# One step of a softplus moved from VectorE to ScalarE, and a buffer of its own for B and C

## The chip, the cores and the metric

The kernel runs on one core of a Trainium2 chip. Its engines take instructions from queues of their own, in order, and wait for one another by semaphores: TensorE (PE; its weight loads are PEld), VectorE (DVE), ScalarE (ACT), GpSimd (POOL) and SyncE (SP), which here only issues DMAs. SBUF is the on-chip memory, and PSUM the memory that TensorE writes its products to. The metric is device microseconds of one execution, lower is better.

## What is computed

Two layers act on x, (4, 128, 64, 64) in fp32. Layer 0 is a selective scan over four orders of the pixels (rows, columns, and both reversed); layer 1, an additive attention and a recurrence, is not touched. Of layer 0 the part that matters, for each image and each of the K = 4 orders:

```python
dt = softplus(dts + dt_bias)           # per channel and pixel
def step(h, inp):                      # along the L = 4096 pixels of the order
    ut, dtt, bt, ct = inp
    dA = jnp.exp(dtt[..., None] * A)   # N = 16 states per channel
    h = dA * h + (dtt * ut)[..., None] * bt
    y = jnp.sum(h * ct, axis=-1)
    return h, y
```

The kernel takes the softplus of s as relu(s) + ln(1 + e), with e = exp(-|s|). In fp32, 1 + e is rounded; to make up for that it adds the error of the rounding, e - ((1 + e) - 1). So four terms are summed: e, relu(s), minus ((1 + e) - 1), and ln(1 + e).

## The kernel before, in words

Layer 0 is cut into 64 items: 4 images by 4 orders (i = 0 to 3) by 4 chunks of CH = 1024 pixels. An item is 16 units, v = 0 to 15, each a pair of (four of the 16 states) by (32 of the 128 channels), so that one unit fills 128 partitions by 1024. The text below calls item m's units v0, v1 and so on.

One unit u goes through the engines so. `decay` (L624): ACT writes dA = exp(dt * A) to a PSUM tile `pa`, of which there are two. `entering` (L629): POOL writes dBu = dtdu * B to one of three buffers. `scan` (L644): DVE runs the recurrence along the 1024 pixels, with the last column of the item before (`carry`) as its start; then, in 10 of 16 units, DVE multiplies by C into a buffer `h` (L651); in the other 6, v2, v5, v7, v10, v13 and v15, the scan writes `h` itself and POOL multiplies it by C (L654). There are five `h` buffers. ACT copies the last column to `carry` (L652), and the POOL multiplication comes after that copy. `collect` (L669 and L671): once per two units TensorE adds their `h` into the sum `py`; the first two of an item (after v3 and v5) also add the skip term or the order before (L669). `deliver` (L678, at v2) copies the finished sum of the item before out of `py`.

Beside that, one step per unit, the inputs of item m + 2 are prepared during item m (the tuple `Item.STEPS`, L594):

- v0 `inputs`: TensorE projects B and C. v1 `outputs` (L554): ACT copies them to `bc`, and a DMA on SP's queue (L556) writes `bc` to DRAM, from where it is spread to all partitions later (L607).
- v2 `raw`: TensorE projects s. v3 `signs` (L567, L568): ACT takes |s| to `e` and relu(s) to `dd`. v4 `power` (L571): ACT makes e = exp(-|s|).
- v5 `first`: TensorE starts a sum in PSUM with identity * e and identity * dd.
- v6 `second`: DVE makes `ec` = (e + 1) - 1 (L579), then ACT overwrites e with ln(1 + e) (L580).
- v7 `third`: TensorE adds `nident` * ec, where `nident` is minus the identity, and identity * ln.
- v8 `products`: DVE multiplies by the source (L588), ACT copies dt (L590), and a DMA on SP's queue (L592) writes both to DRAM; four spreads per item (L599) bring them back for the units.

`bc` and `ec` share one buffer (tag "ec" of a pool with one buffer per tag): `bc` of one item may not be overwritten by `ec` before its DMA has read it.

All of this stands in one order written out by hand: the loop at L781 issues, for each unit u, decay(u+1), entering(u+2), perhaps `deliver`, the step of `STEPS` and other work put beside it (the layer's ending for the image before, normalisation and convolutions for the next), then scan(u), its `carry` copy and POOL's multiplication, then perhaps `collect`, then the DMAs. Each engine runs its share of that order in sequence.

Ahead of the loop, items 0 and 1 are prepared without overlap (L710 to L719): all steps of item 0, its spreads (24 DMAs, of which 16 are spreads of dt and 8 of B and C), then all steps of item 1, then four ACT copies that transpose the image (L454) with four DMAs (L460), and then the first `decay`.

Of the kernel before, what the change touches and what calls it, by code (L numbers as in the profile page):

```python
# [8 lines left out]
F32 = mybir.dt.float32  # L9
AF = mybir.ActivationFunctionType  # L10
ALU = mybir.AluOpType
# [4 lines left out]
P = 128  # L16
# [4 lines left out]
CH = 1024  # L21
K = 4
N = 16
# [121 lines left out]
@with_exitstack  # L145
def _bounded(
    ctx: ExitStack,
    tc: tile.TileContext,
    flag,
    x1,  # L150
    x, in_wT, conv_w, conv_b, sa_w, sa_b, xpT, xpR, dtwT, dtb, A_quads, Ds,
    on_g, on_b, n1_g, n1_b, out_wT, WtT, WxT, Wt, Wx, bh, Wa, ba, W, WT, VT, gamma, beta,
    out,
):
    nc = tc.nc
    const = ctx.enter_context(tc.tile_pool(name="fconst", bufs=1))
    dram = ctx.enter_context(tc.tile_pool(name="gdram", bufs=1, space=DRAM))
    k = _Consts(tc, const)
    x2 = dram.tile([B, P, L], F32, name="x2")

    with tc.manual_schedule():
        _layer0(tc, k, x, x1, in_wT, conv_w, conv_b, sa_w, sa_b, xpT, xpR, dtwT, dtb, A_quads, Ds,
                on_g, on_b, n1_g, n1_b, out_wT)
    top = const.tile([P, TOPS], F32, name="top")
    with tc.manual_schedule():
        _rational(tc, k, x1, x2, top, Wt, Wx, bh, Wa, ba)
    with tc.tile_pool(name="gresid", bufs=1) as resid:
        X = resid.tile([P, B, L], F32, name="X")
        for b in range(B):
            nc.sync.dma_start(X[:, b, :], x2[b])  # L170
        _chunked(tc, None, flag, top, X, k.ident, k.avg, k.ones, k.eps5, k.load, k.filled,
                 W, WT, VT, gamma, beta, out)
# [3 lines left out]
def _layer0(ctx, tc, k, x, x1, in_wT, conv_w, conv_b, sa_w, sa_b, xpT, xpR, dtwT, dtb, A_quads, Ds,  # L176
# [8 lines left out]
    nc = tc.nc  # L185
    load, filled, ident, avg, ones, eps5, eps6 = k.load, k.filled, k.ident, k.avg, k.ones, k.eps5, k.eps6
    wp = ctx.enter_context(tc.tile_pool(name="l0w", bufs=1))
# [7 lines left out]
    def pq():  # L195
        return psQ.tile([P, MM], F32, name="pq", tag="pq")
# [30 lines left out]

    skip = wp.tile([P, P], F32, name="skip")
    nc.vector.tensor_scalar(skip, ident, d_sum, None, ALU.mult)
    nident = wp.tile([P, P], F32, name="nident")  # L230
    nc.vector.tensor_scalar(nident, ident, -1.0, None, ALU.mult)


    gmat = filled(wp, [P, P], 0.25, "gmat")
# [62 lines left out]
    pp = ctx.enter_context(tc.tile_pool(name="l0prep", bufs=1))  # L297
# [13 lines left out]
    def banks(lhsT, src, start=True, stop=True, into=None):  # L311

        into = into or [pq() for _ in parts]
        if lhsT is not None:
            for ps, m in zip(into, parts):
                nc.tensor.matmul(ps, lhsT, src[:, m], start=start, stop=stop)
        return into
# [212 lines left out]
    class Item:  # L530
# [18 lines left out]
                nc.tensor.matmul(ps[0 : 2 * N, :], w_xp[:, self.i, :], self.src[:, m], start=True, stop=True)  # L549

        def outputs(self):
            bc = pp.tile([2 * N, CH], F32, name="bc", tag="ec")
            for ps, m in zip(self.ps, parts):
                nc.scalar.copy(bc[:, m], ps[0 : 2 * N, :])  # L554
            self.bcd = dram.tile([2 * N, CH], F32, name="bcd")
            nc.sync.dma_start(self.bcd, bc)  # L556
# [16 lines left out]
        def first(self):  # L573
            self.ps = banks(ident, self.e, stop=False)
            banks(ident, self.dd[:, 0, :], start=False, stop=False, into=self.ps)

        def second(self):
            self.ec = pp.tile([P, CH], F32, name="ec", tag="ec")
            nc.vector.tensor_scalar(self.ec, self.e, 1.0, 1.0, ALU.add, ALU.subtract)  # L579
            nc.scalar.activation(self.e, self.e, AF.Ln, bias=1.0)  # L580

        def third(self):
            banks(nident, self.ec, start=False, stop=False, into=self.ps)
            banks(ident, self.e, start=False, into=self.ps)

        def products(self):
# [5 lines left out]
            nc.sync.dma_start(self.ddd.rearrange("s d l -> d s l"), self.dd)  # L592

        STEPS = (inputs, outputs, raw, signs, power, first, second, third, products)  # L594

        def spread_dt(self, r):
# [1012 lines left out]
```

## Time and profile before

| what | value |
|---|---|
| three runs | 11802.34, 11821.63, 11826.4 us; median 11821.63 |
| the profiled execution | 11810.23 us, its span 11808.5 us |
| span taken by layer 0 | to about 4069 us; its loop of units starts at 220.8 us |
| DVE, ACT, POOL, PE busy from 2000 to 3000 us | 906.47, 554.10, 865.69, 759.90 us |
| period of one item | 50.5 to 68.5 us; 55.8 us for many |
| L579 on DVE | 64 times, 149.4 us; shortest 664, median 1328, longest 7178 ns |

A row of the timeline gives the start and the duration in us, the engine, the line, the operation, output<-input with shapes, and in brackets how long the engine had been idle before it and what ended the wait. An item's period is the distance from its first scan to the next item's first scan. A duration may contain time in which the instruction was held up after it had been started.

### The profile page before, as it was taken

Reading aid. Unit: us, or ns where it says so; the run is one execution under the profiler, and the core shown is the slowest. Engines: PE = TensorE matmul, PEld = TensorE weight load, DVE = VectorE, ACT = ScalarE, POOL = GpSimd, SP = SyncE. Lnnn points to the kernel's source line nnn. Section 1 sums busy time; section 2 is a strip of 40 time slices with the busy share of each in tenths; the row PEclk is TensorE's granted clock in tenths of the full one; section 3 lists DMA queues with packets and bytes.
Section 4 is the critical chain, followed back from the end, with each engine's and each line's share of the span. In section 5 each row is a group of like instructions: output and inputs, shape, how many; then the busy total and the mean of one; then the engine's idle time right before and its main releaser. Section 6 shows DMA issues by size and latency. Waiting matters only on the chain.

```text
span 11808.5 us, 111596 instructions
## 1 busy us (share of the span) xinstructions
PE 10343.2 (88%) x36083; PEld 3200.5 (27%) x36083; DVE 9180.8 (78%) x10131; ACT 9429.7 (80%) x10096; POOL 8599.9 (73%) x3648
## 2 busy tenths in 40 slices
PE   5687787677776699999999999999999999999986
PEld 2121122122111133333333333333333333333324
DVE  4999899889989677777777777777777777777763
ACT  3455555555555599999999999999999999999985
POOL 2898889889889677767767776767677667767751
PEclk8898898889888899999999999999999999999998
DMA  4778778778778300000000000000000000000001
GB/s 107 180 180 193 172 175 187 171 174 188 178 168 189 87 1 3 6 3 3 6 3 3 3 6 3 3 3 6 3 3 6 3 2 3 4 2 2 4 17 43
DMA packets 224900, 737.83 MB, mean 62 GB/s; under 512 B 41056, under 2 KB 42016, under 8 KB 223792
## 3 DMA queue, kind: packets, MB, share of 16 engines
q1 hardware_dynamic: 221184, 729.96, 26.2%
q8 instruction: 285, 4.67, 0.2%
q14 instruction: 311, 2.55, 0.1%
q10 hardware_dynamic: 3120, 0.64, 0.0%
HBM read 613.01 MB, written 117.44 MB: 62 GB/s over the span
## 4 chain that ended last, share of the span: by engine, by line
PE 49%; ACT 10%; DVE 4%; issue 3%; POOL 0%; DMA 0%; DVEq 0%; POOLq 0%; SPq 0%; ACTq 0%
PE pn L1215 26%; PE pd L1215 15%; ACT A L1384 3%; PE ct L1360 3%; ACT A L1385 2%; DVE rb L1230 2%; ACT rb L1234 1%; ACT rb L1235 1%; PE ct L1137 1%; ACT ra L1234 1%; PE wxs L1501 0%; DVE A L1346 0%; DVE rb L1242 0%; PE pn L55 0%; PE ct L1265 0%
## 5 line engine op out<-in xcount | busy, mean ns | idle before, releaser
L1215 PE MATMUL pn<-cE,F 32*128 32x512 f32 (+1 forms) x12288 | 4724.9, 649 | 193.1 <-DVE rb L1230 85.4
L1230 DVE TENSOR_TENSOR rb<-rb,pn 128x512 f32<-128x512 f32 x3972 | 2543.1, 682 | 1310.3 <-PE pd L1215 684.2
L1215 PE MATMUL pd<-E,F 32*128 32x512 f32 (+1 forms) x12288 | 3474.6, 648 | 24.7 <-DVE ra L1242 19.5
L1349 POOL TENSOR_TENSOR ra<-ra,rb 128x1024 f32<-128x1024 f32 x993 | 2634.3, 2653 | 953.1 <-DVE rb L1230 952.7
L1336 POOL TENSOR_TENSOR ra<-ra,rb 128x1024 f32<-128x1024 f32 x993 | 2347.5, 2364 | 407.1 <-DVE rb L1230 347.2
L629 POOL TENSOR_TENSOR dBu<-dtdu,bbcc 128x1024 f32<-128x1024 f32 x1024 | 2398.2, 2368 | 273.8 <-DMA dtdu<-ddd 154.1
L1235 ACT ACTIVATE rb<-rb 128x1024 f32<-128x1024 f32 x1986 | 2100.3, 1058 | 62.8
L1215 PEld LDWEIGHTS pn<-cE,F 32*128 32x128 f32 (+1 forms) x12288 | 1416.3, 185 | 2571.4 <-DVE rb L1230 1067.5
L1234 ACT ACTIVATE rb<-pd 128x1024 f32<-128x1024 f32 x1986 | 2007.7, 1011 | 83.2 <-PE pn L1215 69.9
L671 PE MATMUL py<-h,gather 128*32 128x512 f32 x4096 | 1304.2, 702 | 479.7 <-POOL h L654 381.8
L1230 DVE TENSOR_TENSOR ra<-ra,pn 128x512 f32<-128x512 f32 x1986 | 1315.6, 683 | 230.3 <-ACT ra L1235 183.9
L1215 PEld LDWEIGHTS pd<-E,F 32*128 32x128 f32 (+1 forms) x12288 | 930.6, 185 | 1642.4 <-issue 884.3
L624 ACT ACTIVATE pa<-dtdu,a_neg 128x1024 f32<-128x1024 f32 x1024 | 1144.9, 1118 | 52.4 <-DVE h L644 31.3
L654 POOL TENSOR_TENSOR h<-h,bbcc 128x1024 f32<-128x1024 f32 x384 | 924.1, 2406 | 351.2 <-ACT carry L652 343.7
L644 DVE TENSOR_TENSOR_SCAN pa<-pa,carry,dBu 128x1024 f32<-128x1024 f32 x480 | 1125.2, 2344 | 21.8 <-ACT pa L624 11.3
L1235 ACT ACTIVATE ra<-ra 128x1024 f32<-128x1024 f32 x993 | 1049.5, 1057 | 31.4
L1360 PE MATMUL ct<-A,xT 128*128 128x512 f32 x2048 | 1046.8, 639 | 11.1 <-ACT A L1385 11.0
L1234 ACT ACTIVATE ra<-pd 128x1024 f32<-128x1024 f32 x993 | 1008.8, 1016 | 59.4 <-PE pd L1215 27.4
L652 ACT COPY carry<-pa 128x1 f32<-128x1 f32 x640 | 102.4, 160 | 1120.8 <-DVE h L651 1119.4
L1346 DVE TENSOR_TENSOR A<-ra 128x512 f32<-128x512 f32 x993 | 743.4, 749 | 116.1 <-POOL ra L1336 115.7
L651 DVE TENSOR_TENSOR h<-pa,bbcc 128x1024 f32<-128x1024 f32 x640 | 783.8, 1225 | 60.4 <-DVE pa L644 1.8
L644 DVE TENSOR_TENSOR_SCAN h<-pa,carry,dBu 128x1024 f32<-128x1024 f32 x288 | 674.9, 2343 | 124.1 <-PE py L671 80.4
(286 smaller groups left out, 8832.5 us busy)
## 6 DMA issues: line engine op xcount, KB each, us to landing
bbcc<-bcd SPq DMA_DIRECT2D x1024, 256.0 KB, 7.0
dtdu<-ddd SPq DMA_DIRECT2D x1024, 256.0 KB, 7.1
ddd<-dd SPq DMA_DIRECT2D x64, 1024.0 KB, 5.1
src<-src SPq DMA_DIRECT2D x64, 512.0 KB, 8.1
xs<-in_x_dram SPq DMA_DIRECT2D x16, 512.0 KB, 7.5
src<-xs SPq DMA_DIRECT2D x16, 512.0 KB, 3.0
bcd<-bc SPq DMA_DIRECT2D x64, 128.0 KB, 2.1
src<-xsT SPq DMA_DIRECT2D x16, 512.0 KB, 4.4
```

The lines of the kernel that those rows point to most:

```text
L624: nc.scalar.activation(dA, its[m].DT[r][:, 0, :], AF.Exp, scale=a)
L629: nc.gpsimd.tensor_tensor(dBu, its[m].DT[r][:, 1, :], its[m].BC[q][:, 0, :], ALU.mult)
L644: nc.vector.tensor_tensor_scan(to[:, step], dA[:, step], live.pop(("dBu", u))[:, step], 0.0 if m % nch == 0 else its[m - 1].carry[:, col : ...
L654: nc.gpsimd.tensor_tensor(h, h, cc, ALU.mult)
L671: nc.tensor.matmul(it.y[to, c], gather, live["h", v][:, c], start=False, stop=(q == QS - 1))
L1215: nc.tensor.matmul(ps[a], F[lo:hi, i, jt * P : (jt + 1) * P], side[lo:hi, i, :], start=True, stop=True)
L1230: nc.vector.tensor_tensor(r[:, a, :], r[:, a, :], ns[a], ALU.mult)
L1234: nc.scalar.activation(r, d, AF.Ln, scale=LOWER)
L1235: nc.scalar.activation(r, r, AF.Exp, scale=-1.0)
L1336: nc.gpsimd.tensor_tensor(rA_, rA_, rB2_, ALU.add)
L1349: nc.gpsimd.tensor_tensor(rA, rA, rB1, ALU.add)
L1360: nc.tensor.matmul(ct, xT[:, jt, :], A[:, jt, :], start=(jt == 0), stop=(jt == JT - 1))
```

## The change

`second` loses its DVE instruction. In its place `first` issues two ScalarE activations after its matmuls: ec = 1 + e, and then ec = 1 - ec, which is minus ((1 + e) - 1). So `third` multiplies by the plain identity, and `nident` is gone. `bc` gets a buffer of its own.

```diff
-    nident = wp.tile([P, P], F32, name="nident")
-    nc.vector.tensor_scalar(nident, ident, -1.0, None, ALU.mult)
...
         def outputs(self):
-            bc = pp.tile([2 * N, CH], F32, name="bc", tag="ec")
+            bc = pp.tile([2 * N, CH], F32, name="bc")
...
             self.ps = banks(ident, self.e, stop=False)
             banks(ident, self.dd[:, 0, :], start=False, stop=False, into=self.ps)
 
+            self.ec = pp.tile([P, CH], F32, name="ec")
+            nc.scalar.activation(self.ec, self.e, AF.Identity, bias=1.0)
+            nc.scalar.activation(self.ec, self.ec, AF.Identity, scale=-1.0, bias=1.0)
+
         def second(self):
-            self.ec = pp.tile([P, CH], F32, name="ec", tag="ec")
-            nc.vector.tensor_scalar(self.ec, self.e, 1.0, 1.0, ALU.add, ALU.subtract)
             nc.scalar.activation(self.e, self.e, AF.Ln, bias=1.0)
 
         def third(self):
-            banks(nident, self.ec, start=False, stop=False, into=self.ps)
+            banks(ident, self.ec, start=False, stop=False, into=self.ps)
             banks(ident, self.e, start=False, into=self.ps)
```

In the built program's order of instructions, DVE lacks the 64 `ec` instructions and `nident`, ACT has 128 more and no further table load, and TensorE's, POOL's and SP's lists keep their length and order. On ACT the two stand between the decay of v6 and the carry copy of v5.

## The prediction, made before the changed kernel was run

> **What bounds the kernel now.** The slices come first, since the share of the whole span hides where the edit lies.
>
> ```profile
> DVE  4999899889989677777777777777777777777763
> ACT  3455555555555599999999999999999999999985
> POOL 2898889889889677767767776767677667767751
> ```
>
> Layer 0 is slices 1 to 14. There DVE and POOL are full and ACT is half idle, so work seems to be moved from a bound engine to a free one. But two engines are near full, and which of them ends an item has to be read per item. Next, the group and the waits of DVE (220 to 3985 us):
>
> ```profile
> L579 DVE TENSOR_SCALAR ec<-e 128x1024 f32<-128x1024 f32 x64 | 149.4, 2335 | 48.4 <-DMA bcd<-bc 35.5 <-ACT e L571 13.0
> ```
>
> ```profile
> DVE h L644 <- PE py L671: 94.3, 62, 3.9
> ```
>
> L579 takes 2335 ns in the mean, yet 664 at its shortest. Item by item, of the 62 inside the loop 28 take 0.66 to 0.67 us, 19 take 1.1 to 2.1, and 15 take 6.3 to 7.2. And DVE also waits for TensorE 62 times, always for an `h` buffer. Three places in the timeline tell what the durations mean. Item 17 (order i = 0):
>
> ```profile
> 1208.27 1.12 ACT L624 ACTIVATE pa<-dtdu,a_neg 128x1024 f32<-128x1024 f32 x1
> 1210.22 6.59 DVE L579 TENSOR_SCALAR ec<-e 128x1024 f32<-128x1024 f32 x1
> 1211.58 2.38 POOL L654 TENSOR_TENSOR h<-h,bbcc 128x1024 f32<-128x1024 f32 x1
> 1213.89 2.36 POOL L629 TENSOR_TENSOR dBu<-dtdu,bbcc 128x1024 f32<-128x1024 f32 x1
> 1216.73 2.35 DVE L644 TENSOR_TENSOR_SCAN pa<-pa,carry,dBu 128x1024 f32<-128x1024 f32 x1
> 1219.15 2.36 POOL L629 TENSOR_TENSOR dBu<-dtdu,bbcc 128x1024 f32<-128x1024 f32 x1 [2.90 <-DVE pa L644]
> 1220.32 2.34 DVE L644 TENSOR_TENSOR_SCAN h<-pa,carry,dBu 128x1024 f32<-128x1024 f32 x1
> ```
>
> L579 is held until POOL stops: POOL's last ends at 1216.25, L579 at 1216.81, 0.56 later. POOL stops only for lack of a dBu buffer, which the scan queued behind L579 would free: each holds up the other. Item 30 (i = 3):
>
> ```profile
> 1999.03 1.37 DVE L579 TENSOR_SCALAR ec<-e 128x1024 f32<-128x1024 f32 x1
> 1999.81 2.93 POOL L654 TENSOR_TENSOR h<-h,bbcc 128x1024 f32<-128x1024 f32 x1
> 2005.57 1.06 PE L671 MATMUL py<-h,gather 128*32 128x512 f32 x4
> 2006.76 2.35 DVE L644 TENSOR_TENSOR_SCAN h<-pa,carry,dBu 128x1024 f32<-128x1024 f32 x1 [2.77 <-PE py L671]
> ```
>
> Here the scan of v7 waits 2.77 us for TensorE's second sum, which ends at 2006.63. And the preparation of item 1, ahead of the loop:
>
> ```profile
> 195.49 0.31 SPq L556 DMA_DIRECT2D bcd<-bc  x1
> 204.22 0.69 DVE L579 TENSOR_SCALAR ec<-e 128x1024 f32<-128x1024 f32 x1 [35.45 <-DMA bcd<-bc]
> 204.97 3.78 PE L316 MATMUL pq<-ec,nident 128*128 128x512 f32 x4 [20.91 <-DVE ec L579]
> 220.78 2.30 DVE L644 TENSOR_TENSOR_SCAN pa<-pa,dBu 128x1024 f32<-128x1024 f32 x1 [8.64 <-ACT pa L624]
> ```
>
> `ec` waits for the shared buffer until the DMA has read `bc`, and that DMA stands on SP's queue behind 24 spreads. The whole loop starts late for it.
>
> **What the Trainium skill says.** "SBUF — State Buffer", Who interferes with whom: DVE in a mode that reads one tensor through both its ports locks the port pair that is GpSimd's only one, for the whole instruction, and the loser blocks fully; ACT waits for nobody. The trace agrees (the 0.56 us above; POOL's 2.93 beside its usual 2.36). The page's "whoever starts first" doesn't tell why 15 cases last through several POOL instructions; that stays open, but all of them go with the instruction. "ScalarE: Activation LUTs", What ACT_TABLE_LOAD costs: 186 + 0.833 ns per column with immediate scale and bias, an estimate of 1039 ns for 1024 columns, and 93 more per pointer operand; L571, of that form, has 1039 as its shortest, and L504, with two pointers, about 1245. "Perfetto Trace Analysis", Optimizing Scalar/DVE Operations: with DVE saturated, offloading to ScalarE may pay. That depends here on which engine comes next.
>
> **Part 1, the buffer.** After the change item 1 doesn't wait. Its matmuls of `first` end at 184.06 (181.13 + 2.93), and `ec` is ready before: exp ends at 177.5, and two activations of 1.06 give 179.6. `third` starts at 184.06 instead of 204.97, and everything down to the first scan follows it: 20.9 us earlier, at 199.9. Next late is the DMA queue. It isn't free before 204.2; in the fill each MB of spread takes 4.8 us (POOL's first three inputs land at 184.81, 189.49, 194.41). Ahead of the spread of B and C for v8 stand ddd (1 MB), four image stores (2 MB), one spread of dt (1 MB) and that spread itself. Stores show up to 400 GB/s in this stretch, so 3 + 6 + 4.8 + 0.6 + 4.8 = 19 us: it lands at about 223, and POOL asks for it at 242.4 - 20.9 = 221.5. A stall of 1.5, perhaps as much again for item 1's: I keep 18, with 10 and 21 as ends.
>
> **Part 2, L579 out of DVE, by kind of item (62 in the loop).**
> - 15 long ones. Eight are of order 0 (items 1, 3, 16, 17, 32, 33, 48, 49). In item 17 DVE would be ready for v6 6.6 us earlier, and TensorE's second sum (ending 1214.6) lets v7 start at 1214.7, not 1220.32: 5.6. Then v8 waits for the products, whose TensorE step comes after that sum: in item 30 v7 to v8 is 4.15 us, here it was 3.43, so 4.9 stay. The same on item 32 gives 4.6; items 1 and 3 may fall from 56.8 to the 51.9 or so that POOL needs, 4.9. Sum 3 x 4.9 + 3 x 4.6 + 2 x 4.9 = 38.3. The other seven are of orders 1 and 3. There TensorE's second sum comes as in item 30, v8 at 31.2 us after the item's start instead of 32.5: 1.25 each, 8.7.
> - 5 that POOL paces (items 2, 56 to 59). Item 58: period 52.2, POOL busy 51.5, its one idle 0.58 before v10's multiplication. That goes, DVE being early; POOL's 0.48 of hold goes too, but the carry copy before its v5 multiplication comes 0.3 later. About 0.5 each, 2.5.
> - 42 others. In nearly all v7 already waits 0.2 to 3.6 us for TensorE (item 0 aside), whose chain (deliver, sum, first, sum) has no step on DVE at v6. DVE saves 0.67 to 1.4 us and waits as much longer. Zero; at most 0.3 each, 12.
>
> **Part 3, what ACT gets.** 62 pairs at 2 x 1.06 = 2.1 us; with two pointers each they would be 2.5. ec's second waits for its first, as L1235 does for L1234, where 1.06 us lie between starts. Queued behind are the carry copy of v5, the decay of v7 and ln. In item 30 ACT sat idle 1.44 us ahead of that copy, in item 34 3.42, in item 17 0.95: the copy comes 0 to 1.2 us late. POOL's v5 multiplication is behind it: it started at 1211.58 with the copy done at 1210.52, and would find it done at 1211.7 (the decay ends at 1209.4, then 2.1 and 0.2), so 0.1 late. Decay of v7 ends by 21.5 us after the item's start, v7 starts at 23 or later. ln is needed after TensorE's second sum: hidden. I take zero beyond the 0.3 above; the bounds are 0 and 1.2 x 62 = 74, all of it passed on.
>
> `nident` and the plain identity: one small DVE instruction less in the set-up, beside the weights' DMAs: zero. SP's and POOL's queues keep their order.
>
> **Sum.** 18 + 38.3 + 8.7 + 2.5 = 67.5 us, 0.57%. Against the profiled execution, 11810.2 - 67.5 = 11742.7. That one lies 11.4 below the median of three; the mean of all four executions is 11815.2, so I say 11748.
>
> **Rivals.**
> - A, the whole group counts: 149.4 + 20.9, giving 11645. For it: DVE at nine tenths. Against it: the wait for TensorE at v7, and POOL at 51.5 of 52.2. 3%.
> - B, the long stalls are only an adjustment: without them POOL, the DMAs (90% of the time busy in item 30) or the layer's ending take the room, and 15 x 1.25 + 18 + 2.5 = 39 are left: 11776. For it: POOL idles by 6 us later in item 17, behind ACT's carry, so something else paces that half. 17%.
> - C, slower: the pair at the head of ACT's queue. At 2.5 us and a further 0.2 for its inner wait, less the 0.95 idle of items 17 and 58, the carry copy of v5 is 1.75 late; if POOL passes that on in each of 62 items, 108 us, more than the 65 of the stalls and the fill: + 43, so 11858. It ends on the slow side from (65 + 24) / 62 = 1.44 us per item on. Against it: idle of 1.4 to 5.8 in most items, and v7's wait beyond. 4%.
> - D, no effect: the fill's gain is given back to the DMA queue and carries cost what the stalls gave; 11800 to 11840. 6%.
>
> **Chances.** The forecast 70%: 11722 (the fill at 21, the zeros at 12, and 11 of scatter, the runs' 0.1%) to 11768 (the fill at 10, 12 of scatter). What a measurement of this kernel can tell from no change is 0.2%, 24 us. Faster: forecast, A and B, 89%; same 7%; slower 4%. The range goes up to B and its scatter with some 7 us more, 11795, and down to 11712, 10 below the forecast's own, for the long stalls of orders 1 and 3, whose 1.25 each is read from neighbours and not from their own rows.
>
> **What would show it.** First scan near 200 us and the wait for bcd gone; items 1, 3 at 52, items 17, 33, 49 at 61 to 62, item 30 still 55.8 with v7's wait near 4 us. No POOL row of 2.9 us. Wrong if POOL's L654 waits for the carry of v5 in the order-0 items, if the fill's POOL waits 5 us or more for bcd's spread, or if the 66 us items keep their length.

## The result, and the profile after

The changed kernel takes 11745.52 us (median of four runs, 11743.34 to 11746.66), the kernel before 11818.28 (four runs, 11802.34 to 11826.4): a ratio of 0.9938, 95% interval 0.9925 to 0.995. The prediction said 11748. From profiled execution to profiled execution it is 11810.23 - 11743.34 = 66.9 us, where the prediction's sum was 67.5.

First the slices of the page, changed kernel. Layer 0 is again slices 1 to 14.

```profile
DVE  4998899889889577777777777777777777777763
ACT  3566556656655599999999999999999999999985
POOL 3999799889889577677767766766777667667751
```

ACT has gone from 5 to 5 or 6 tenths in layer 0, and POOL's first slice from 2 to 3. DVE hardly looks emptier, although L579 with its 149.4 us has gone: its busy time over the whole span fell from 9180.8 to 9044.2 us. The two lines on layer 0 that show more are the scan that writes `h` (page, costliest groups: busy, mean ns, idle before and releaser), and DVE's waits from 201 to 3915 us (total, times, longest):

```profile
L644 DVE TENSOR_TENSOR_SCAN h<-pa,carry,dBu 128x1024 f32<-128x1024 f32 x288 | 675.0, 2344 | 171.3 <-PE py L671 148.5
```

```profile
DVE h L644 <- PE py L671: 200.8, 97, 4.5
```

The wait for TensorE was 94.3 us, 62 times, and is 200.8, 97 times. DVE gave back 148 us of L579 inside the loop and waits 107 us more for TensorE. In the 42 items to which the prediction gave zero, that wait grew by 64.5 us: L579 had taken 36.8 there, and a wait of such scans for POOL's dBu, 31.2 us in ten of them, is gone. Most of the rest, 28.1, lies in the seven long items of orders 1 and 3, where L579 had taken 48.4. Item 30, the same place as in the timeline of before (starts and durations):

```profile
1951.79 1.04 ACT L576 ACTIVATE ec<-e 128x1024 f32<-128x1024 f32 x1
1952.86 1.06 ACT L577 ACTIVATE ec<-ec 128x1024 f32<-128x1024 f32 x1
1953.83 0.17 ACT L652 COPY carry<-h 128x1 f32<-128x1 f32 x1
1954.08 2.47 POOL L654 TENSOR_TENSOR h<-h,bbcc 128x1024 f32<-128x1024 f32 x1
1959.70 1.06 PE L671 MATMUL py<-h,gather 128*32 128x512 f32 x4
1960.89 2.35 DVE L644 TENSOR_TENSOR_SCAN h<-pa,carry,dBu 128x1024 f32<-128x1024 f32 x1 [4.06 <-PE py L671]
```

The wait of v7 has grown from 2.77 to 4.06 us, by about the 1.37 of L579; the period is 55.81 us, and was 55.84. POOL's multiplication L654 takes 2.47 and no longer 2.93, and none of POOL's L629 and L654 in the whole layer takes over 2.56. Item 17, one of the long ones, started at 1151.27 us:

```profile
1170.59 1.04 ACT L576 ACTIVATE ec<-e 128x1024 f32<-128x1024 f32 x1
1171.49 2.33 DVE L644 TENSOR_TENSOR_SCAN pa<-pa,carry,dBu 128x1024 f32<-128x1024 f32 x1
1171.67 1.06 ACT L577 ACTIVATE ec<-ec 128x1024 f32<-128x1024 f32 x1
1172.63 0.17 ACT L652 COPY carry<-h 128x1 f32<-128x1 f32 x1
1172.91 2.37 POOL L654 TENSOR_TENSOR h<-h,bbcc 128x1024 f32<-128x1024 f32 x1
1175.24 4.66 POOL L629 TENSOR_TENSOR dBu<-dtdu,bbcc 128x1024 f32<-128x1024 f32 x2
1176.01 2.35 DVE L644 TENSOR_TENSOR_SCAN h<-pa,carry,dBu 128x1024 f32<-128x1024 f32 x1 [0.86 <-PE py L671]
1178.69 0.69 DVE L588 TENSOR_TENSOR dd<-src,pq 128x512 f32<-128x512 f32 x1 [0.33 <-PE pq L314]
1180.15 2.35 DVE L644 TENSOR_TENSOR_SCAN pa<-pa,carry,dBu 128x1024 f32<-128x1024 f32 x1
```

v7 starts 24.74 us after the item, not 30.67, and POOL goes on without the pause of 2.90. Of those 5.9 us v8 keeps 5.2, since it now has 4.14 us behind v7 with the products (L588) between them, where it had 3.42. The pair on ACT delays nothing here: the copy ends at 1172.80, and POOL is busy with three earlier instructions, a run of 6.99 us from 1165.95, until 1172.94. Last the fill, preparation of item 1:

```profile
181.78 1.06 ACT L576 ACTIVATE ec<-e 128x1024 f32<-128x1024 f32 x1
182.87 1.06 ACT L577 ACTIVATE ec<-ec 128x1024 f32<-128x1024 f32 x1
188.19 1.88 PE L314 MATMUL pq<-ec,ident 128*128 128x512 f32 x4
199.80 0.31 SPq L554 DMA_DIRECT2D bcd<-bc  x1
201.22 2.30 DVE L644 TENSOR_TENSOR_SCAN pa<-pa,dBu 128x1024 f32<-128x1024 f32 x1 [8.71 <-ACT pa L624]
```

`ec` is written long before the DMA of `bc` is issued at 199.80. TensorE adds it from 188.19 on and not from 204.97, and the first scan starts at 201.22, where it started at 220.78. Of these 19.6 us 16.8 are `third`'s earlier start. The other 2.8 come after it: from `third` to the projection behind it (L547, L549 before) it took 4.1 us (188.19 to 192.33) at a granted TensorE clock of 1.00, and 6.9 before (204.97 to 211.85) at 0.59.

Cut at the first and the last scan of layer 0, the profiled executions give this:

| us | before | after | difference | predicted |
|---|---|---|---|---|
| first scan, less what item 0 gives back | 220.8 + 50.7 | 201.2 + 53.0 | -17.3 | -18 |
| eight long items of order 0 | 497.6 | 460.4 | -37.2 | -38.3 |
| seven long items of orders 1 and 3 | 406.3 | 392.4 | -13.9 | -8.7 |
| items 2 and 56 to 59, paced by POOL | 263.5 | 261.3 | -2.2 | -2.5 |
| 42 others | 2494.7 | 2495.0 | +0.3 | 0 |
| from the last scan to the end | 7826.5 | 7829.6 | +3.1 | 0 |

With -0.1 for the last, cut-off item the sum is -67.2, the difference of the spans.

### The profile page after: what moved, and what is told of

Its sections match the earlier page's. It is cut to its first block, busy times and chain, and to the rows that moved or that the text cites. A ratio compares the mean times of both kernels' runs of the same rounds, so it can differ in the third digit from the quotient of the medians.

```text
span 11741.3 us, 111542 instructions
## 1 busy us (share of the span) xinstructions
PE 10349.8 (88%) x36083; PEld 3206.7 (27%) x36083; DVE 9044.2 (77%) x10066; ACT 9555.0 (81%) x10224; POOL 8586.9 (73%) x3648
## 4 chain that ended last, share of the span: by engine, by line
PE 49%; ACT 10%; DVE 4%; issue 3%; POOL 0%; DMA 0%; DVEq 0%; POOLq 0%; SPq 0%; ACTq 0%
PE pn L1215 26%; PE pd L1215 15%; PE ct L1360 3%; ACT A L1384 3%; ACT A L1385 2%; DVE rb L1230 2%; ACT rb L1234 1%; ACT rb L1235 1%; PE ct L1137 1%; ACT ra L1234 1%; DVE rb L1242 1%; PE wxs L1501 0%; DVE A L1346 0%; PE ct L1265 0%; PE pn L55 0%
## 5 line engine op out<-in xcount | busy, mean ns | idle before, releaser
L629 POOL TENSOR_TENSOR dBu<-dtdu,bbcc 128x1024 f32<-128x1024 f32 x1024 | 2397.7, 2366 | 219.8 <-DMA dtdu<-ddd 158.5
L654 POOL TENSOR_TENSOR h<-h,bbcc 128x1024 f32<-128x1024 f32 x384 | 911.4, 2373 | 346.8 <-ACT carry L652 337.8
```

What stands on the lines that cost most here:

```text
L629: nc.gpsimd.tensor_tensor(dBu, its[m].DT[r][:, 1, :], its[m].BC[q][:, 0, :], ALU.mult)
L654: nc.gpsimd.tensor_tensor(h, h, cc, ALU.mult)
```

## Experiments

In all of them the ratio is to the kernel before, run beside them on the same chip; its medians were 11810.27 to 11814.69 us. "Layer 0" below is the start of the last scan, "the loop" the time from the first to the last scan, both from one profiled execution of each.

**The two parts by themselves.** The kernel before with only the buffer:

```diff
-            bc = pp.tile([2 * N, CH], F32, name="bc", tag="ec")
+            bc = pp.tile([2 * N, CH], F32, name="bc")
```

> The kernel before with a buffer of its own for bc alone; ec stays on VectorE. My account (fill and loop are separate gains): the loop starts near 200 instead of 220.8 us, item 0 gives back some 2 us to the DMA queue, the 15 long ec instructions stay at 6.3 to 7.2 us: 17 us less than before, ratio 0.9985. The rival that the DMA queue eats the fill's gain: less than 5 us. The rival that the shared buffer also caused the long instructions in the loop: long ones vanish, 60 us or more.

Measured: 11805.66 us, ratio 0.9991 (0.9984 to 0.9997). And the changed kernel with one buffer for both again:

```diff
-            bc = pp.tile([2 * N, CH], F32, name="bc")
+            bc = pp.tile([2 * N, CH], F32, name="bc", tag="ec")
...
-            self.ec = pp.tile([P, CH], F32, name="ec")
+            self.ec = pp.tile([P, CH], F32, name="ec", tag="ec")
```

> The changed kernel with bc and ec in one buffer again; ec on ScalarE. My account: the loop's items are those of the changed kernel (order-0 long items 51.6, 57, 61 us), 53 us less than before; ahead of the loop ScalarE now waits for bc's DMA until about 204 us, then needs two activations, so the loop starts 1 to 2 us later than before, at about 222. Net 51 us less than before, ratio 0.9957. With the first run's 17 it makes up the whole, about 68. Rival, that the two parts need each other: less than 40 us, or ScalarE waits for the buffer inside the loop too.

Measured: 11772.86 us, ratio 0.9964 (0.995 to 0.9977). By their totals the parts give 9 and 42, together 51, where both give 73, or 69 against the runs used here (11814.69): some 20 us are missing (30 between the profiled executions). In layer 0 none are: the last scan comes 22.9 us earlier with the buffer and 47.8 with the pair, together 70.7, and with both 70.3. What is missing lies behind it, in code that all these kernels share: from the last scan to the end it took 7844.4 and 7842.4 us, against 7826.5 and 7829.6 before and after. So the parts add up as far as one execution of each can tell (15 long items in the kernel before, 14 with the buffer alone; see below for what that is worth), and a difference of under some 18 us between totals of these kernels can't be put down to layer 0 unseen. It seems to go with the kernel and not with the execution: two profiles of the kernel before have 7826.5 and 7827.6 us there. Where those 18 come from is only partly clear: in the first 25 us after the last scan the granted clock of TensorE was 0.86 before, 0.66 after and 0.60 in these two, which goes with 4 to 6 us there; the rest builds up in small jumps along layer 1. Its cause stays open.

**What ACT's pair costs.** The changed kernel with a second, useless pair behind the first, into the half of `dd` that is free at that time:

```diff
             nc.scalar.activation(self.ec, self.ec, AF.Identity, scale=-1.0, bias=1.0)
+            nc.scalar.activation(self.dd[:, 1, :], self.e, AF.Identity, bias=1.0)
+            nc.scalar.activation(self.dd[:, 1, :], self.dd[:, 1, :], AF.Identity, scale=-1.0, bias=1.0)
```

> The changed kernel with a second pair of the same activations behind the first, into a part of dd that is free then; the results aren't used. ScalarE gets 2.1 us more per item at v5. My account: ScalarE has slack in most items, and only those that POOL paces or whose v7 comes at 23 us (items 1 to 3, 16, 17, 32, 33, 48, 49, 56 to 59) pay, 1.5 to 2 us each: 20 to 26 us more than the changed kernel, ratio to before about 0.996. Rival, ScalarE's queue at v5 is on the path everywhere: 2.1 x 62 = 130 us more, slower than before. Rival, it is nowhere on the path: within 5 us of the changed kernel.

Measured: 11751.35 us, ratio 0.9945 (0.9931 to 0.9958): 6 us above the changed kernel, and in the loop 3713.6 against 3710.5, so 3. The 2.1 us per item at the head of ACT's queue would be 130 if they were on the path. My 20 to 26 was too much as well: I had the copy of v5 late in every item, and POOL lets most of that pass. POOL's waits of this kernel, from 200 to 3915 us:

```profile
POOL h L656 <- ACT carry L654: 358.1, 184, 6.0
```

The same wait was 343.7 us before and 337.8 after. One pair adds nothing to it, a second one 20 us; but then POOL waits less for DVE's scan, 27.1 instead of 52.9, and little is left of it in the time.

**Lock, or DVE's time?** The change takes two things from DVE: an instruction's time, and the lock over which it and POOL hold each other up (6.59 us for L579 in item 17, 2.93 for POOL's L654 in item 30). The Trainium skill, "SBUF — State Buffer", Who interferes with whom, excepts the `tensor_scalar` "form that also writes out its accumulator" from those that can take the shared port pair. So L579 was left on DVE in that form, with a buffer of its own. It makes ec = e, so this kernel leaves out the correction of the rounding:

```diff
-            nc.vector.tensor_scalar(self.ec, self.e, 1.0, 1.0, ALU.add, ALU.subtract)
+            spare = small.tile([P, 1], F32, name="spare")
+            nc.vector.tensor_scalar(self.ec, self.e, 1.0, 0.0, ALU.mult, ALU.add, accum_out=spare)
```

> The kernel before with bc's own buffer, and ec on VectorE in the form that also writes its accumulator; it computes ec = e, so the correction of the rounding is left out. If the long stalls come from the port pair that this form doesn't take, ec takes about the same 1.2 to 1.3 us everywhere (estimate [...]as for L651), POOL's rows of 2.9 us are gone, and the order-0 long items fall by 4 or more: 45 to 65 us less than before, though ec is still on VectorE. If instead VectorE's own time is what counted, or VectorE and POOL hold each other in any form, it gains only the 17 of the buffer.

Measured: 11747.0 us, ratio 0.9942 (0.9928 to 0.9955), the time of the changed kernel (11745.52). DVE's groups of this kernel in layer 0:

```profile
L580 DVE TENSOR_SCALAR_CACHE_REDUCE ec<-e 128x1024 f32<-128x1024 f32 x62 | 74.0, 1194 | 0.0
L580 DVE DVE_READ_ACCUMULATOR ec<-e 128x1 f32 x62 | 5.1, 83 | 0.0
```

DVE still spends 79 us here. But none of the 62 is held, and the loop is 3707.1 us, as short as with ACT's pair. So it was the hold that cost in this kernel, not DVE's time, and the trace agrees with the skill's exception. The trade is clear in the numbers: this form takes 1194 ns alone where the plain one takes 664, and costs less.

**Which items are long?** The kernel before, once more:

> The kernel before once more, for a second profile. If the long stalls are drawn anew in each execution (its runs lie 24 us apart, those of the changed kernel 3), other items show the 6 to 7 us than items 1, 3, 4, 12, 15 to 17, 28, 32, 33, 44, 47 to 49 and 60, and layer 0 has another length by some 5 to 15 us. If they are fixed by the program, the same items do.

Measured: 11828.91 us, a single run. Its long items aren't the same: 20 of 62, among them 2, 29, 39, 54, 56, 57, 59 and 61, which were short in the first profile, and without 12, 33 and 48, which were long. In the kernel with only the buffer there were 14, again others. The loop took 3758.3 us with 14 long ones, 3761.2 with 15 and 3774.3 with 20. So which items are long isn't fixed by the code alone, though it isn't free either: 12 of the 15 were long again. In these three profiles L579 started during a POOL instruction in 34, 34 and 35 of the 62 items, and only among these is it ever held; where POOL was idle at its start it took at most 0.68 us. The runs show the draw too: those of the kernel before scatter by 24 us (four runs) and by 33 (nine runs), those with only the buffer by 23, and those of the changed one by 3.

**Behind the wait at v7.** In the 42 items the saving went into the wait for TensorE. Can it be had? Two ways: a sixth `h` buffer, so that v7 needn't wait for TensorE's second sum; and the scan of v8 put ahead of the step with the products, which wait for TensorE's `third`. First the buffer only (a small tile moved to another pool makes the room):

```diff
-    ph = ctx.enter_context(tc.tile_pool(name="l0h", bufs=5))
+    ph = ctx.enter_context(tc.tile_pool(name="l0h", bufs=6))
...
-                self.pool = small.tile([P, 2, HH // 2 + 4], F32, name="pool")
+                self.pool = big.tile([P, 2, HH // 2 + 4], F32, name="pool")
```

> The changed kernel with six h buffers instead of five (a small tile is put elsewhere to make room). In the items of orders 1 and 3 the scan of v7 should no longer wait 4.1 us for TensorE's second sum. My account: the wait only moves, since DVE's products, which stand ahead of v8, need TensorE's sums that come after the second collect: v8 stays at 31.2 us after the item's start, the period at 55.8; within 8 us of the changed kernel. Rival, that the h buffer alone paces these items: they fall to 52 to 53, 60 us or more less.

Measured: 11745.87 us, ratio 0.9941 (0.9927 to 0.9954): nothing. Item 30 of this kernel:

```profile
1954.41 2.35 DVE L644 TENSOR_TENSOR_SCAN h<-pa,carry,dBu 128x1024 f32<-128x1024 f32 x1
1961.73 0.69 DVE L588 TENSOR_TENSOR dd<-src,pq 128x512 f32<-128x512 f32 x1 [4.97 <-PE pq L314]
```

v7 starts 4.6 us earlier, and the products behind it wait 4.97. Then the order only, with five buffers:

```diff
+            if v == 8:
+                scan(u)
             for _, go in sorted(steps, key=lambda x: x[0]):
                 go()
-            scan(u)
+            if v != 8:
+                scan(u)
```

> The changed kernel with five h buffers and only the scan of v8 put ahead of the step. Theory (two waits stand one behind the other, at v7 for the h buffer and at v8 for the products, and removing one of them leaves the other to set the period, as more h buffers alone did): within 15 us of the changed kernel's 11745. Rival (the products at v8 are the wait that counts, and v7's is only where slack gathers): most of the 132 us that both edits gave, so 11640 or less. In between, the wait at v7 moves v8 to 28.4 us after an item's start instead of 30.2: 1.8 in some 50 items, 11655.

Measured: 11742.41 us, ratio 0.9946 (0.9929 to 0.9963): 3 us under the changed kernel, next to nothing. Item 30 again:

```profile
1959.31 2.35 DVE L644 TENSOR_TENSOR_SCAN h<-pa,carry,dBu 128x1024 f32<-128x1024 f32 x1 [4.06 <-PE py L671]
1961.58 2.33 DVE L644 TENSOR_TENSOR_SCAN pa<-pa,carry,dBu 128x1024 f32<-128x1024 f32 x1
```

Now the products don't hold up v8, which starts 29.3 us after the item and not 31.2; but v7 waits its 4.06 us as ever, and the products' 1.27 us follow behind v8. The period is 55.2 us, 0.6 less. Then both:

> The same with the scan of v8 ahead of the step of v8, so that the products come after that scan. If TensorE's chain at v7 and the products at v8 are what paces orders 1 and 3, and POOL comes next at 51.6, then v9 starts near 31 instead of 34.8 us, and some 23 items fall from about 56 to 52.5: 60 to 90 us less than the changed kernel, near 11670. Rival, that DVE or DMA paces them anyway: less than 20 us.

Measured: 11613.18 us, ratio 0.9829 (0.9816 to 0.9842), 132 us under the changed kernel, more than the 60 to 90 that I expected. In item 30 neither scan waits for TensorE any more:

```profile
1895.12 2.35 DVE L644 TENSOR_TENSOR_SCAN h<-pa,carry,dBu 128x1024 f32<-128x1024 f32 x1
1897.86 2.36 DVE L644 TENSOR_TENSOR_SCAN pa<-pa,carry,dBu 128x1024 f32<-128x1024 f32 x1 [0.38 <-POOL dBu L629]
```

Its period falls from 55.8 to 52.2 us, and the 42 items together from 2495.0 to 2404.3. The two waits stand for one chain of TensorE, met at two places; either edit alone leaves the other place to set the period. The third way leaves five buffers and shortens the chain: `first` keeps only ACT's pair, ln goes to the free half of `dd`, all four parts of the sum follow each other in `third`, and v8 goes first as above:

```diff
         def first(self):
-            self.ps = banks(ident, self.e, stop=False)
-            banks(ident, self.dd[:, 0, :], start=False, stop=False, into=self.ps)
...
         def second(self):
-            nc.scalar.activation(self.e, self.e, AF.Ln, bias=1.0)
+            nc.scalar.activation(self.dd[:, 1, :], self.e, AF.Ln, bias=1.0)
 
         def third(self):
+            self.ps = banks(ident, self.e, stop=False)
+            banks(ident, self.dd[:, 0, :], start=False, stop=False, into=self.ps)
             banks(ident, self.ec, start=False, stop=False, into=self.ps)
-            banks(ident, self.e, start=False, into=self.ps)
+            banks(ident, self.dd[:, 1, :], start=False, into=self.ps)
```

> The changed kernel with five h buffers, all four terms of the softplus summed at v7 (first keeps only ScalarE's pair; ln goes to the half of dd that is free then), and the scan of v8 ahead of the step of v8. TensorE's second collect then comes 3.7 us earlier, v7 at 23.3 instead of 27.0 us in orders 1 and 3. My account: the same gain as six buffers with late products, 60 to 90 us less than the changed kernel. Rival, that the wait goes to the products, now behind 7.3 us of sums: less than 20 us.

Measured: 11627.0 us, ratio 0.984 (0.9827 to 0.9853). Item 30, with v7 22.9 us after the item's start and not 27.0:

```profile
1901.98 2.34 DVE L643 TENSOR_TENSOR_SCAN h<-pa,carry,dBu 128x1024 f32<-128x1024 f32 x1
1904.23 2.33 DVE L643 TENSOR_TENSOR_SCAN pa<-pa,carry,dBu 128x1024 f32<-128x1024 f32 x1
```

The order of v8 alone gave 3 us, so it was TensorE's matmuls of `first`, standing ahead of the second sum, that v7 waited for. With the sixth buffer as well:

> Six h buffers, all four parts of the softplus's sum at v7, and the scan of v8 ahead of the step. Theory (POOL, at 51 us of work an item, is next, and both ways to let DVE through have brought the items to it): within 8 us of 11613. Rival (TensorE's chain still sets some items): 20 us or more below.

Measured: 11585.33 us, ratio 0.9812 (0.9796 to 0.9828), the best of all; 28 us below, so the rival holds: TensorE's chain still set some items, such as items 20, 36 and 52, 65.5, 65.5 and 63.7 us in the kernel without `first`'s matmuls moved and 62.0, 62.1 and 60.3 here. In item 30 (window by engine: length, then PE, PEld, DVE, ACT and POOL busy, TensorE's clock, DMA share, GB/s) POOL is now full, and waits for no DMA, though the DMA engines are 0.98 busy:

```profile
1857.16:1908.03 50.87, 37.04 (x104) 8.84 (x103) 49.65 (x30) 31.06 (x47) 50.05 (x23) 0.87 0.98 236
```

**The change where no wait hides it.** L579 back on DVE, `bc` and `ec` in one buffer as before, with the sixth buffer and v8 first:

> The kernel before (ec on DVE, bc and ec in one buffer) with the two edits of the kernel with six h buffers and the scan of v8 ahead of the step: what the change is worth once DVE no longer waits for TensorE at v7 and for the products at v8. Theory (the change gained little in 42 items only because a wait for TensorE stood behind L579): here each of the 62 instructions is on the path, 62 x 1.0 to 1.4 us, beside the long stalls, some 15 x 5, and the fill's 20: 60 to 85 + 75 + 20, so 155 to 180 above 11613, about 11770 to 11795. Rival (POOL paces the odd-order items anyway, and only stalls and fill count): 95 above, about 11708.

Measured: 11728.28 us, ratio 0.9931 (0.9914 to 0.9947). And the same with the accumulator form, which leaves out the correction:

> The kernel before with six h buffers and the scan of v8 ahead of the step, and L579 in the form that also writes an accumulator (it makes ec = e, so the correction of the rounding is left out); bc and ec share a buffer as in the kernel before. Against the same kernel with the plain form it tells what the port lock costs, and against the one with ScalarE's pair what 1.2 us of DVE time per item cost there. Theory (the lock is the stalls, DVE's time counts once the wait for TensorE is gone): the fill's 20 and up to 62 x 1.2 = 74 above 11613, so 11680 to 11705, and some 75 below the plain form. Rival (POOL paces, DVE's time is slack there too): 11633 to 11645.

Measured: 11658.44 us, ratio 0.9875 (0.9858 to 0.9891). The loops take 3687.8 (plain), 3593.0 (accumulator) and 3578.8 us (ACT's pair). So the hold costs 95 us between these executions, and the late first scan (223.4, 222.6 and 199.2) 23 to 24. DVE's time costs 14, or 18 without item 0, which gives back 3.5 of the fill: part of the accumulator form's 79 us of DVE time, between the 74 of that run's theory and the nothing of its rival. By medians the plain and the accumulator form are 70 apart, since the profiled execution of the plain one was the slowest of its four, which lie 31 us apart. My theory that each L579 would now be on the path falls, and the rival, POOL's pace, is nearer. Two neighbouring items of the plain form show the hold by itself. Item 30, period 52.2 us:

```profile
1961.44 2.35 POOL L629 TENSOR_TENSOR dBu<-dtdu,bbcc 128x1024 f32<-128x1024 f32 x1
1962.91 1.44 DVE L579 TENSOR_SCALAR ec<-e 128x1024 f32<-128x1024 f32 x1
1963.75 2.92 POOL L654 TENSOR_TENSOR h<-h,bbcc 128x1024 f32<-128x1024 f32 x1
```

Item 31, period 57.1 us:

```profile
2013.88 2.34 POOL L629 TENSOR_TENSOR dBu<-dtdu,bbcc 128x1024 f32<-128x1024 f32 x1
2014.79 6.75 DVE L579 TENSOR_SCALAR ec<-e 128x1024 f32<-128x1024 f32 x1
2016.19 2.41 POOL L654 TENSOR_TENSOR h<-h,bbcc 128x1024 f32<-128x1024 f32 x1
2018.57 2.40 POOL L629 TENSOR_TENSOR dBu<-dtdu,bbcc 128x1024 f32<-128x1024 f32 x1
2023.87 2.36 POOL L629 TENSOR_TENSOR dBu<-dtdu,bbcc 128x1024 f32<-128x1024 f32 x1 [2.90 <-DVE pa L644]
```

In item 30 L579 gets in at the end of POOL's running instruction (1963.79) and POOL's next is held, 2.92 instead of 2.4. In item 31 POOL's next two go first, and L579 ends 0.57 us after the last of them. The difference is 4.9 us of period. There are 18 such items in this execution. Item by item against the accumulator form, these 18 are longer by 4.0 to 5.8 us each, together 93.0, and all others by 2.0.

## Why the prediction was right, point by point

- **The bound.** Two full engines, but a wait for TensorE that decides most items: held. In the 42 items DVE lost 36.8 us of work and they kept their length, with 64.5 us more of that wait. With both of its places cleared, the change and the sixth buffer with the order together give 200 us against the kernel before (11813 to 11613). By itself the change gives 73, and the two edits on the kernel before give 82 (11810 to 11728): they help each other by some 45 us.
- **The fill.** 18 predicted, 17.3 found: the first scan 19.6 earlier, 2.3 given back in item 0. The stall for B and C's spread came as worked out: POOL waits for it until 226.49, 1.82 us against the 1.5 of the sum. That the sum is so near is luck in part. The set-up ahead of `third` ran 4.2 us later in this execution (exp of item 1 at 180.69, before at 176.44, in the second profile of the kernel before at 181.00), so `third` came at 188.19 and not at 184.06, and the 2.8 us that the quicker TensorE gave made up for most of it. Over all profiles the first scan starts at 220.8 to 225.3 with the shared buffer and at 198.6 to 201.2 with two.
- **Order 0's long items.** 38.3 against 37.2. Items 1 and 3 are 51.6, items 17, 33 and 49 61.2, 61.5 and 62.8. The sum held better than its parts: items 17, 33 and 49 gave 5.2, 4.5 and 3.2 for 4.9 each, items 1 and 3 5.2 each for 4.9. Why item 49 gave so little isn't shown; with the accumulator form on DVE it is 61.2 us long. The step "v7 to v8 is 4.15 us, so 4.9 stay of 5.6" is easily left out, and it held (4.14).
- **Orders 1 and 3.** 8.7 against 13.9: the one term mis-sized. I took v8 at 31.2 us after the item's start from item 30. In items 4, 12, 28, 44 and 60 v7 comes at 26.1 and v8 at 30.2, since their chain of TensorE is 0.9 ahead of item 30's: 2.2 each, not 1.25. Items 15 and 47 gave 1.4 each.
- **The 42 others.** Zero against +0.3 in the sum (single items moved by up to 1.3 us either way), with v7's wait at 4.06 in item 30, as forecast ("near 4 us").
- **ACT's pair.** Zero, and its cover has room: a second pair cost 3 to 6 us. The skill's "Perfetto Trace Analysis", Optimizing Scalar/DVE Operations, that offloading from a full DVE may pay, gives the right sign here for another reason than a full DVE: a form that stays on DVE without the lock does as well.
- **The rivals.** A (11645, the whole group counts) fell with the wait at v7. B (11776, the long ones only an adjustment) fell with item 17. C (slower, ACT's queue) fell with POOL's wait for the copy, 343.7 before and 337.8 after. D fell with the first scan and with item 0, which gave back 2.3 of 19.6. (In the chances forecast, A and B add up to 90%, not 89.)
- **Not seen.** The prediction took the 15 long items as fixed by the code. They are in part drawn, 15 and 20 in two executions. Had the profiled one been that with 20, the same working would have promised more. So the mechanism was right, but that 67.5 met 66.9 is luck in part: the 5.2 us too few for orders 1 and 3 are balanced by 1.8 too many for the fill and order 0 and by the 3.1 that the code behind layer 0 took longer, to which the prediction gave nothing.

What stays open: why L579 gets in at one boundary between POOL's instructions and not at the next. In the kernel before, the held ones came where the copy that releases POOL's next instruction had ended 0.69 to 1.55 us ahead of the running one's end, and most that got in at 0.27 to 0.6; but five got in at 0.78 to 1.26. In the second profile some were held from 0.46 on and others got in up to 1.52, so that alone doesn't decide it.

## What to carry to other kernels

An instruction whose mean is far above its shortest may be held: read it item by item, ask what its holder waits for, and look for a form or an engine that doesn't take the shared resource before counting its busy time as the gain. Where one chain is waited for at two places of a queue, an edit at either place alone measures as nothing; clear both before giving up. A gain no larger than what the code behind it varies by is read from the stage that was edited, not from the total.

## What the runs showed of the hardware

- A plain DVE `tensor_scalar` on 128x1024 fp32 takes 0.66 to 0.68 us inside the loop when POOL is idle at its start, up to 2.4 when it gets in at the next boundary between POOL's instructions, and 6.0 to 7.2 when it doesn't and POOL goes on until it has no free dBu buffer (four profiles, 14 to 20 of 62 held). The Trainium skill, "SBUF — State Buffer", Who interferes with whom, lets whoever issues first have the pair; here two POOL instructions that started after L579 ran ahead of it, in item 31 above as in every held case, and which items it hits differs in part from execution to execution.
- The form with accumulator takes 1194 ns plus 82 for its readout, and none of 62 was held.
- Two dependent ACT activations of 1024 columns start 1.07 to 1.14 us apart, 1.08 in the mean of 64.
- The same code after layer 0 took 7826.5 to 7844.4 us in profiled executions of different kernels, and 7826.5 and 7827.6 in two of the same kernel; the cause is open.
